# Where the first state of a chunk reads delta*x in a selective-scan kernel

## The chip, the cores and the metric

The kernel runs on one core of one Trainium2 chip. The metric is the device time of one execution in microseconds. The core has five engines that run side by side, each through its own queue in order: PE (matrix products), DVE (vector), ACT (scalar functions and copies), POOL (GpSimd, elementwise work here) and SP (which issues the DMAs). SBUF is the working memory, PSUM the small memory that PE writes to; DVE and ACT can read and write both[...].

## The reference, cut to what matters

The whole is a two-layer network on four images of 64 x 64 positions with 128 channels. The first layer begins with a selective scan over 4096 positions in four directions; the change lies there. The other parts (routing and experts, a long convolution through short transforms) run beside the scans or after them.

```python
def step(h, xs):
    ut, dt, bt, ct = xs
    dA = jnp.exp(dt[..., None] * A)
    h = dA * h + (dt * ut)[..., None] * bt[:, :, None, :]
    y = jnp.einsum('bkdn,bkn->bkd', h, ct)
    return (h, y)
```

Here `u` is x along a direction, `dt` (delta) the step size, and `h` has N = 16 states for each of 256 inner channels. The term `(dt * ut)` is delta*x: it does not depend on the state n, and each of the 16 states multiplies it by its own row of B.

## The kernel before

The sequence of an image and direction is cut into chunks of 512 positions: 4 images x 4 directions x 8 chunks are 128 chunks. A chunk lies in tiles of 128 partitions x 2 halves x 512 positions. The main loop runs over `s`, which counts (chunk, state) pairs: 128 x 16 = 2048 steps. At step `s` it emits work for several pairs at once:

- for pair s+5 the DMA of its B and C rows into `bc`, L1402, on SP;
- for pair s+3 the decay `da` = exp(delta * A), two ACT instructions, L1412;
- for pair s itself, on DVE: the product `db` = delta*x * B into PSUM, L1440, then two scans (one per half) that give `hh`, L1446. A chunk that continues a sequence starts from `hst`, the states kept from the chunk before;
- for pair s-1, on POOL: the copy of the last column to `hst`, L1455, and the product `hh` * C, L1456;
- for pair s-2, on PE: eight transposing matmuls that add up `y` in PSUM, L1482, and after the chunk's last state two ACT copies of `y`, L1352.

The step sizes of a chunk are made in pieces while the chunk before is scanned (`step_sizes`): PE L1311, ACT L1315 to L1338, POOL L1337 to L1344. They give `dl` (delta) and, as the last piece, `dx` = delta*x on POOL (L1344), in SBUF, with a single buffer. At the last state of a chunk, `into_psum` has ACT copy the next chunk's `dx` into `du` in PSUM, one copy per half (L1393). `du` has a single buffer too, so the copies can only be written when the last product of the old chunk has been read. All 16 products of a chunk read `du`:

```python
nc.scalar.copy(dus[i][:, h, :], sizes[i][1][:, h, :])                            # L1393
nc.vector.tensor_mul(db, dus[i], bcs[s][:, 0:1, :].to_broadcast([P, 2, SC]))     # L1440
```

Other work of the network is dealt out between the steps (`deal`): it is queued behind the instructions of the step at hand, a fixed share per step, and none at states 2 and 3 of a chunk. So ACT's queue holds, beside `da` and the copies, silu parts, norms and evictions of that side work. Within these limits the framework's scheduler decides the order on each engine. After the last scan comes a tail without scans: the rest of the long convolution and of the experts.

Of the kernel before, what the change touches and what calls it, by code (L numbers as in the profile page):

```python
# [17 lines left out]
P = 128  # L18
# [10 lines left out]
SC = 512  # L29
# [49 lines left out]
def kernel(  # L79
# [35 lines left out]
    nc = tc.nc  # L115
# [106 lines left out]
    def settle(leave=0):  # L222
        while len(soon) > leave:
            soon.pop(0)()
# [1030 lines left out]
    def run(pieces):  # L1255
        for _ in pieces:
            tick()
        flush()
# [3 lines left out]
    def beside(b):  # L1262

        if b == 0:
            for i in range(1, B):
                yield from before_scans(i)
            for i in range(B - 1):
                yield from gate(i)
            yield from filters()
        else:  # L1270
            yield from after_scans(b - 1)
            yield from experts_and_sums(b - 1)
            yield from to_slots(b - 1)
            if b == 1:
                yield from gate(B - 1)
            if b == B - 1:
                yield from from_slots(0)
            yield from convolve(all_groups[BESIDE * (b - 1) : BESIDE * b])

    with ExitStack() as c0:  # L1280
# [102 lines left out]
        sizes = {0: step_sizes(0, 0, 0)}  # L1383
        list(sizes[0][3])
        bcs, das, hhs, dus, hsts, ys = {}, {}, {}, {}, {}, {}
# [3 lines left out]
        def into_psum(i):  # L1389

            dus[i] = bps.tile([P, 2, SC], F32, name="du")
            for h in range(2):
                nc.scalar.copy(dus[i][:, h, :], sizes[i][1][:, h, :])  # L1393

        for s in range(-5, total + 2):
            i = max(s, 0) // N
# [22 lines left out]
            if 0 <= s < total:  # L1419
                b, k, step, _ = chunks[i]  # L1420
                n = s % N
                if n == 0:
                    if k == 0 and step == 0:
                        y_d[b] = dram.tile([K, L, DI], F32, name=f"y_d{b}")
                        if b > 0:
                            run(share["pieces"])
                            settle()
                        share = {"pieces": beside(b), "made": 0.0, "due": 0.0}
                    hsts[i] = pb.tile([P, 2, N], F32, name="hst") if step == 0 else hsts[i - 1]
                    if i == 0:  # L1430
                        into_psum(0)
                if i + 1 < len(chunks):
                    if n == 1:
                        nb_, nk, _, nci = chunks[i + 1]
                        sizes[i + 1] = step_sizes(nb_, nk, nci)
                    if n >= 1:
                        next(sizes[i + 1][3], None)
                hhs[s] = pb.tile([P, 2, SC], F32, name="hh", bufs=6)
                db = bps.tile([P, 2, SC], F32, name="db")
                nc.vector.tensor_mul(db, dus[i], bcs[s][:, 0:1, :].to_broadcast([P, 2, SC]))  # L1440
                for h in range(2):
                    init = 0.0 if step == 0 else hsts[i][:, h, n : n + 1]
                    o, d0, d1 = hhs[s][:, h, :], das[s][:, h, :], db[:, h, :]
                    if k >= 2:
                        o, d0, d1 = o[:, ::-1], d0[:, ::-1], d1[:, ::-1]
                    i_dve = nc.vector.tensor_tensor_scan(o, d0, d1, init, ALU.mult, ALU.add)  # L1446
                if n == N - 1 and i + 1 < len(chunks):
                    into_psum(i + 1)
# [14 lines left out]
            c, n = divmod(t, N)  # L1463
# [163 lines left out]
```

## Time and profile before

| what | value |
| --- | --- |
| median of 3 runs | 11200.73 us (11200.63 to 11202.45) |
| profiled execution | 11189.8 us |
| its span, first to last instruction | 11188.0 us |
| DVE busy | 8145.9 us (73% of the span) |
| POOL busy | 7262.3 us (65%) |
| PE busy | 8372.3 us (75%) |
| ACT busy | 6173.9 us (55%) |
| products L1440 | 2048, mean 1232 ns |
| scans L1446 | 3584 of mean 1266 ns and 512 of mean 1208 ns |
| copies `du` L1393 | 256, median 590 ns |
| POOL's products L1456 | 2048, mean 2359 ns |

In the profile a row of a group names line, engine, operation, output<-inputs and count, then the busy time and the mean duration of one, then how long its engine had stood idle before it and what ended most of that. The view of waits gives, for a pair of waiting and released-by instructions, the total in us, the number of times and the longest. The timeline gives start and duration in us; in brackets stands the idle time before an instruction and what ended it. Neighbouring instructions of one kind are merged.

### The profile page before, as it was taken

Reading aid. Unit: us, or ns where it says so; the run is one execution under the profiler, and the core shown is the slowest. Engines: PE = TensorE matmul, PEld = TensorE weight load, DVE = VectorE, ACT = ScalarE, POOL = GpSimd, SP = SyncE. Lnnn points to the kernel's source line nnn. Section 1 sums busy time; section 2 is a strip of 40 time slices with the busy share of each in tenths; the row PEclk is TensorE's granted clock in tenths of the full one; section 3 lists DMA queues with packets and bytes.
Section 4 is the critical chain, followed back from the end, with each engine's and each line's share of the span. In section 5 each row is a group of like instructions: output and inputs, shape, how many; then the busy total and the mean of one; then the engine's idle time right before and its main releaser. Section 6 shows DMA issues by size and latency. Waiting matters only on the chain. (4 is left out here: it accounts for less than half of the span.)

```text
span 11188.0 us, 117102 instructions
## 1 busy us (share of the span) xinstructions
PE 8372.3 (75%) x34656; PEld 4820.6 (43%) x34656; DVE 8145.9 (73%) x7046; ACT 6173.9 (55%) x12043; POOL 7262.3 (65%) x6518
## 2 busy tenths in 40 slices
PE   6677676546766777657677776576677789999999
PEld 2444443334454444444543344455344444355443
DVE  0898988887887999879878898798699933222222
ACT  4667566657566665674655566647456534124222
POOL 1878787888787878788877788778687821001001
PEclk9787777757776888778778887687788899999999
DMA  2465656657556666657565566574666664553555
GB/s 98 161 206 178 200 174 209 191 179 217 203 200 185 187 193 193 201 174 240 172 185 168 170 194 205 159 262 155 188 193 193 189 155 125 150 136 94 143 131 123
DMA packets 901458, 1980.14 MB, mean 177 GB/s; under 512 B 101563, under 2 KB 415579, under 8 KB 899291
## 3 DMA queue, kind: packets, MB, share of 16 engines
q1 hardware_dynamic: 900826, 1972.65, 58.3%
q8 instruction: 283, 4.64, 0.2%
q14 instruction: 349, 2.85, 0.1%
HBM read 1766.77 MB, written 205.52 MB: 176 GB/s over the span
## 5 line engine op out<-in xcount | busy, mean ns | idle before, releaser
L1456 POOL TENSOR_TENSOR hh<-hh,bc 128x1024 f32<-128x1024 f32 x2048 | 4829.5, 2359 | 417.4 <-DVE hh L1446 190.5
L1446 DVE TENSOR_TENSOR_SCAN hh<-da,hst,db 128x512 f32<-128x512 f32 x3584 | 4392.2, 1266 | 528.8 <-PE y L1482 146.6
L1412 ACT ACTIVATE da<-dl,aneg 128x512 f32<-128x512 f32 x4096 | 2765.3, 717 | 2006.7 <-DVE hh L1446 1922.1
L1482 PE MATMUL y<-ident,hh 128*128 128x128 f32 x16384 | 2783.7, 320 | 1092.7 <-POOL hh L1456 980.7
L1482 PEld LDWEIGHTS y<-ident,hh 128*128 128x128 f32 x16384 | 2288.6, 166 | 2452.9 <-POOL hh L1456 1290.6
L1440 DVE TENSOR_TENSOR db<-du,bc 128x1024 f32<-128x1024 f32 x2048 | 2523.2, 1232 | 733.8 <-ACT du L1393 627.3
L1142 PE MATMUL cv_ps<-slab,us 64*128 64x512 f32 x4096 | 1164.0, 674 | 528.0 <-ACT y L256 298.5
L256 ACT COPY y<-cv_ps 128x512 f32<-128x512 f32 (+1 forms) x1024 | 755.3, 742 | 687.3 <-PE cv_ps L1142 658.6
L1163 PE MATMUL zq_ps<-y,me 128*128 128x512 f32 x2048 | 1006.1, 612 | 42.5 <-ACT y L256 37.5
L1455 POOL COPY hst<-hh 128x2 f32<-128x2 f32 x1792 | 338.8, 189 | 1052.4 <-DVE hh L1446 948.1
L1163 PE MATMUL zq_ps<-y,mo 128*128 128x512 f32 x2048 | 973.1, 599 | 0.0
L254 DVE COPY y<-cv_ps 128x512 f32<-128x512 f32 x640 | 441.3, 691 | 559.5 <-PE cv_ps L1142 509.4
L1142 PEld LDWEIGHTS cv_ps<-slab,us 64*128 64x128 f32 x4096 | 398.9, 201 | 981.8 <-ACT y L256 387.2
L1179 POOL TENSOR_TENSOR zt<-zt,zt 128x512 f32<-128x512 f32 x64 | 81.2, 1269 | 1007.3 <-DVE zt L254 531.4
L1446 DVE TENSOR_TENSOR_SCAN hh<-da,db 128x512 f32<-128x512 f32 x512 | 596.9, 1208 | 64.4 <-PE y L1482 29.7
L410 PE MATMUL cv_ps<-xh,diag 128*128 128x512 f32 x1152 | 534.3, 607 | 0.9 <-ACT sg_v L352 0.8
L1163 PEld LDWEIGHTS zq_ps<-y,me 128*128 128x128 f32 x2048 | 353.4, 194 | 379.1 <-issue 266.1
L1163 PEld LDWEIGHTS zq_ps<-y,mo 128*128 128x128 f32 x2048 | 358.3, 192 | 316.2 <-issue 313.3
L1311 PE MATMUL dt_ps<-dts,dtw 8*128 8x512 f32 x512 | 352.8, 804 | 180.7 <-ACT sg_v L352 54.6
L254 DVE COPY zt<-zq_ps 128x512 f32<-128x512 f32 x39 | 26.9, 691 | 529.8 <-PE zq_ps L1163 524.2
L1337 POOL TENSOR_TENSOR ex<-ex,dx 128x1024 f32<-128x1024 f32 x128 | 302.9, 2366 | 147.1 <-ACT dx L1334 146.8
L532 PE MATMUL yk_ps<-yk,ident 128*128 128x512 f32 x512 | 278.4, 689 | 92.1 <-ACT y L256 37.6
(222 smaller groups left out, 8714.4 us busy)
## 6 DMA issues: line engine op xcount, KB each, us to landing
bc<-bc_d SPq DMA_DIRECT2D x2048, 512.0 KB
slab<-hd SPq DMA_DIRECT2D x1024, 256.0 KB
xc<-xc_d SPq DMA_DIRECT2D x128, 512.0 KB
y_d<-ys SPq DMA_DIRECT2D x128, 512.0 KB
w1t<-in_w_dram SPq DMA_DIRECT2D x128, 512.0 KB
w2t<-in_w_dram SPq DMA_DIRECT2D x256, 256.0 KB
xc_x<-xc_d SPq DMA_DIRECT2D x64, 512.0 KB
yk<-y_d SPq DMA_DIRECT2D x128, 256.0 KB
```

The lines of the kernel that those rows point to most:

```text
L254: nc.vector.tensor_copy(dst, src)
L256: nc.scalar.copy(dst, src)
L410: nc.tensor.matmul(ps, diag[:, h, t, :], xh[:, 8 * g + dy : 8 * g + dy + 8, dx : dx + W], start=(t == 0), stop=(t == 8),)
L1142: nc.tensor.matmul(pq[q].rearrange("p (r k t) -> p r k t", r=2, t=BS), us[b, G][rows, p, a if e == 0 else 1 - a, :], slab[i][rows, p, :, : ...
L1163: nc.tensor.matmul(z, (me, mo)[e][:, KQ * kq + k, :], ys[e][:, :, :, :, k, :].rearrange("p a q r t -> p (a q r) t"), start=(e == 0 and k = ...
L1311: nc.tensor.matmul(ps, dtw[:, k, h * P : (h + 1) * P], dts, start=True, stop=True)
L1412: i_act = nc.scalar.activation(das[t][:, h, :], sizes[t // N][0][:, h, :], AF.Exp, scale=aneg[:, tk, h, t % N : t % N + 1],)
L1440: nc.vector.tensor_mul(db, dus[i], bcs[s][:, 0:1, :].to_broadcast([P, 2, SC]))
L1446: i_dve = nc.vector.tensor_tensor_scan(o, d0, d1, init, ALU.mult, ALU.add)
L1455: nc.gpsimd.tensor_copy(hsts[t // N][:, :, t % N], hhs[t][:, :, last])
L1456: i_pool = nc.gpsimd.tensor_mul(hhs[t], hhs[t], bcs.pop(t)[:, 1:2, :].to_broadcast([P, 2, SC]))
L1482: i_pe = nc.tensor.matmul(ys[c][:, q, h, :], hhs[t][:, h, q * P : (q + 1) * P], ident, is_transpose=True, start=(n == 0 and k > 0 and q % ...
```

## The change

The product of a chunk's first state takes delta*x from `dx` in SBUF, where POOL made it. The products of the other 15 states read the copy `du` in PSUM as before; the copies are made as before. With the two added lines, the product stands in line 1442 and the scans in line 1448 of the kernel after.

```diff
                 hhs[s] = pb.tile([P, 2, SC], F32, name="hh", bufs=6)
                 db = bps.tile([P, 2, SC], F32, name="db")
-                nc.vector.tensor_mul(db, dus[i], bcs[s][:, 0:1, :].to_broadcast([P, 2, SC]))
+
+                src = sizes[i][1] if n == 0 else dus[i]
+                nc.vector.tensor_mul(db, src, bcs[s][:, 0:1, :].to_broadcast([P, 2, SC]))
                 for h in range(2):
```

The other lines of the loop, and the functions named above, are the same.

## The prediction

> **What bounds the kernel now.** First the busy times by stretch (span start to 297 us, six stretches of the scan stage up to 9010, then the tail; below, columns are length, then busy time and count for PE, PEld, DVE, ACT and POOL, PE clock, DMA share, GB/s). I show one quiet scan stretch, one crowded one and the tail.
>
> ```profile
> 3660.00:4680.00 1020.00, 758.27 (x3224) 430.74 (x3223) 969.66 (x795) 607.10 (x875) 827.06 (x573) 0.85 0.63 191
> 4680.00:6380.00 1700.00, 1181.54 (x5552) 756.78 (x5552) 1415.75 (x1162) 1016.57 (x2058) 1310.11 (x1205) 0.78 0.60 188
> 9010.00:11188.00 2178.00, 2111.67 (x7100) 940.25 (x7099) 541.18 (x780) 688.77 (x1625) 258.32 (x531) 0.99 0.53 133
> ```
>
> In the quiet stretch DVE works 95% of the time (969.66 of 1020), in the crowded one 83%, and no other engine reaches DVE's share in either. So the scan stage is set by DVE's line of products and scans plus what keeps DVE waiting. The tail is PE's (97% busy); it starts when the last scans are done, so time won before it shifts it whole. The chain that ended last says only this about the tail; it does not reach back into the scans.
>
> Next the view of waits, three rows of it (total us, times, longest):
>
> ```profile
> ACT da L1412 <- DVE hh L1446: 1922.1, 971, 10.3
> POOL hst L1455 <- DVE hh L1446: 948.1, 679, 17.3
> DVE db L1440 <- ACT du L1393: 627.3, 56, 286.6
> ```
>
> ACT and POOL mostly wait for DVE. DVE's own largest wait is for the copy `du`. Of its 627.3 us, 286.6 are the start of the program, before any scan; 340.7 us are 55 waits at chunk boundaries, 6.2 us each. Third, the timeline at one boundary:
>
> ```profile
> 2062.97 2.45 DVE L1446 TENSOR_TENSOR_SCAN hh<-da,hst,db 128x512 f32<-128x512 f32 x2
> ...
> 2067.37 0.60 ACT L1393 COPY du<-dx 128x512 f32<-128x512 f32 x1
> ...
> 2068.51 0.59 ACT L1393 COPY du<-dx 128x512 f32<-128x512 f32 x1
> ...
> 2069.13 1.23 DVE L1440 TENSOR_TENSOR db<-du,bc 128x1024 f32<-128x1024 f32 x1 [3.71 <-ACT du L1393]
> ...
> 2072.98 1.23 DVE L1440 TENSOR_TENSOR db<-du,bc 128x1024 f32<-128x1024 f32 x1
> ```
>
> The last scans end at 2065.42. ACT could copy from 2062.84 on (the old `du` has been read for the last time), but its queue holds side work first, so the copies come at 2067.37 and 2068.51 and DVE stands still for 3.71 us. `dx`, the source of the copies, had been finished by POOL 27.6 us before the last scans ended. From one state's product to the next is 3.85 us (2069.13 to 2072.98).
>
> [...] Today's L1440 has `du` in PSUM[...]; its durations over 2048 are 1205/1232/1233 ns (minimum, median, maximum). Two rows by shape of tiny DVE instructions whose two inputs are both in SBUF[...]:
>
> ```profile
> L626 DVE TENSOR_TENSOR left<-left,hard 128x1 f32<-128x1 f32 x4 | 5.5, 1385 | 0.0
> L629 DVE TENSOR_TENSOR wt<-wt,soft 128x4 f32<-128x4 f32 x1 | 0.1, 132 | 0.0
> ```
>
> The same kind of work costs 132 ns alone and 1385 ns when a POOL instruction is running; in the timeline each long one ends within 0.1 us of that POOL instruction's end, although POOL's next already stands in its queue. [...] No run here shows the new form at this size.
>
> **The change, part by part.** The counts and the operations stay. Only the first product of each of 128 chunks is touched.
>
> *1. The first product's wait goes.* I read, off DVE's and ACT's timelines, when the second `du` copy ended after the last scan at each of 127 boundaries:
>
> - 70 on time: nothing to win.
> - 20 late by up to 3.85 us, together 46.4 us: all of it can be won.
> - 37 late by more, together 355.6 us: here the second product, which still reads `du`, becomes the one that waits. At most one state, 3.85 us, is won: 37 x 3.85 = 142.5.
>
> Sum: 46.4 + 142.5 = 188.9 us of 402. (402 exceeds 340.7 because at five boundaries small routing instructions lie on DVE inside the wait.) What is late next: `dx` itself and `da`. `dx` ends 9 to 47 us before the last scan everywhere but at boundaries 81 to 88, where POOL ends it 1.0 to 7.0 us after; with that and the `da` of the first state counted, some 187 remain.
>
> *2. The port.* At each boundary I took the POOL instruction running when the last scan ends (or `dx` is ready) and let the product wait for its end, as the tiny instructions do. On-time boundaries: 15 of 70 hit, 10.7 us together, longest 1.9. Late ones: 29 us, most of it hidden since the second product waits for `du` anyway. The gain falls from about 187 to **165 us**. Where POOL starts the little `hst` copy (0.19 us) in the same instant, as it does 0.02 to 0.03 us after the product at on-time boundaries, I assume DVE first; bound 0 to 70 x 0.25 = 17 us, or a whole product (2.36) more if POOL slips it in between, which is the rival below.
>
> *3. POOL waits behind the product.* Up to 1.23 us per boundary. Queued behind it are `hst` and the output product L1456, for which PE's transposes wait. POOL needs 0.19 + 2.35 = 2.54 of a state's 3.85 us, so it makes this good in one state. Cost 0, covered by POOL's 948.1 us of waiting for DVE; bound 128 x 1.23 = 157 us if that cover were gone.
>
> *4. The product's own time.* [...] I take 0.
>
> *5. Buffers and queues.* `dx` has one buffer; its next writer is ACT L1334 of the next chunk, now also behind the first product. In the boundary at 2003.85 that writer came at 2021.57, 17.7 us later: cost 0. The 256 copies of 0.59 us stay on ACT, and `du`'s last reader is still state 15. No DMA is added, and none of SP's work is passed by the edit. In the built order the scheduler places about a quarter of the chunks' step-size work (L1311 to L1344) one or two states later (chunk 32: five), still at least five states ahead of its boundary except where it was late already, and ten of the 256 copies half a state to a state away, mostly earlier. I cost this at 0, bound 20 us either way.
>
> *6. What is kept.* A gain stays only if the late copy follows DVE. I walked back from each late copy through what released it. At 47 of 61 boundaries with over 0.3 us of waiting the walk ends at a scan of the chunk just before (states 1 to 14), that is, at work which moves earlier with DVE. The rest end at a DMA, at older work, or can't be followed, and at the five with routing instructions the product stays behind these in DVE's order. I keep three quarters: 0.75 x 165 = 124 us.
>
> **Sum.** The profiled execution took 11189.8 us (span 11188.0, 1.8 around it), 11 us below the median 11200.7. Its span should fall to about 11064; from the median, 11200.7 - 124 = about **11076 us**, 1.1% faster.
>
> **Rivals.**
>
> *The port decides (slower).* [...] Before the port, 0.75 x 187 = 140 us would be won; over 127 boundaries it is gone when a boundary costs 1.1 us more. If POOL's `hst` and L1456 pass first at every on-time boundary, 70 x 2.6 = 182 us are lost, and with 124 won elsewhere the time is about 11259. Against it: waiting instructions got in after one POOL instruction in the trace, and POOL waits for the same scan end as DVE. For it: POOL is 83% busy in the first scan stretch. Chance 0.10.
>
> *The wait only moves.* If the side work's own chain (PE, POOL, DMA) sets when the copy comes, the next boundary is later by what was won. The walk speaks against it, the 14 that do not end at a near scan for it. With under a tenth of 188.9 kept: 11180 to 11201. Chance 0.08. A scheduler that undid the edit would give 11201 too, but the built order has 128 first products that read `dx`, so I give that no chance of its own.
>
> **How the numbers follow.** Main case 0.82. Low end: all 187 kept, without port losses: about 11010. High end: 0.1 x 188.9 kept: about 11180, which takes in half of the case where the wait moves. A measurement of this kernel can tell 0.2%, 22 us, from no change. Faster 0.82, same 0.08, slower 0.10.
>
> **What would show it.** Right: the wait for `du` falls from 340.7 (without the start) to some 215 us and stands before a state's second product; first products sit 0.1 us behind the last scan; their durations reach from 1.2 to about 3.6 us, with some 50 us in all over 1232 ns; a new small wait for `dx` at boundaries 81 to 88. Wrong: first products mostly over 2.4 us, POOL's L1456 lengthened at the boundaries with DVE waiting for `hh` buffers after it, or boundaries late by as much as before.

## The result and the profile after

| | median | range |
| --- | --- | --- |
| before, 4 runs | 11200.68 us | 11198.13 to 11202.45 |
| after, 4 runs | 11129.69 us | 11127.63 to 11149.03 |

The ratio is 0.9941 with an interval of [0.9929, 0.9954]. The change wins 71 us; 124 were forecast. Measured a second time, the same kernel gave 0.9945 [0.9933, 0.9958].

The two profiled executions understate this: that of after took 11149.0 us and is the slowest of its four, while that of before is 11 us below its median. So I also use the profile of the second measurement (below "the repeat", 11130.9 us).

First the same three stretches as before, in the profile after: length, busy time and count of PE, PEld, DVE, ACT and POOL, then PE clock, DMA share and GB/s.

```profile
3660.00:4680.00 1020.00, 773.51 (x3192) 433.40 (x3191) 963.56 (x786) 604.44 (x874) 832.29 (x568) 0.83 0.64 189
4680.00:6380.00 1700.00, 1194.63 (x5627) 757.24 (x5626) 1455.72 (x1179) 1028.97 (x2072) 1345.03 (x1214) 0.78 0.61 190
9010.00:11147.00 2137.00, 2081.81 (x7028) 928.10 (x7026) 535.07 (x771) 679.47 (x1603) 257.20 (x525) 0.99 0.53 132
```

In the crowded stretch DVE's share rises from 83% to 86% (1455.72 of 1700), in the quiet one it is as it was. From the end of the last scan to the end of the program are 2178.7 us, against 2180.8 before: the tail was moved whole.

Next the view of waits of after: total us, times, longest.

```profile
DVE db L1442 <- POOL dx L1344: 313.9, 9, 282.7
DVE hh L1448 <- PE y L1484: 210.5, 62, 20.7
DVE db L1442 <- ACT du L1393: 143.3, 33, 13.2
DVE hh L1448 <- ACT da L1412: 85.0, 38, 7.4
```

The wait for `du` fell from 340.7 (without the start) to 143.3 us, and each of its 31 waits of over 0.2 us stands before the second product of a chunk. The 282.7 us of the `dx` row are the start of the program; the other 31.2 are eight waits, at boundaries 81 to 88 exactly. But DVE's scans wait longer than before for PE (210.5; 176.3 before) and for `da` (85.0; 79.5).

The two rows of the products, on the page of after:

```profile
L1442 DVE TENSOR_TENSOR db<-du,bc 128x1024 f32<-128x1024 f32 x1920 | 2365.8, 1232 | 247.2 <-ACT du L1393 143.3
L1442 DVE TENSOR_TENSOR db<-dx,bc 128x1024 f32<-128x1024 f32 x128 | 222.4, 1738 | 322.6 <-POOL dx L1344 313.9
```

A product that reads `dx` takes 1738 ns in the mean, and so 128 x 0.506 = 64.7 us more than the same products with `du`. In the scan stage, from the first product to the end of the last scan, DVE's idle time falls by 98.4 us (1110.0 to 1011.6) and its busy time rises by 64.0 (7600.2 to 7664.2): the stage is 34.4 us shorter in this profile. In the repeat it is 49.6 us shorter.

The timeline of DVE in after, at the boundary that was shown of before:

```profile
2043.22 2.45 DVE L1448 TENSOR_TENSOR_SCAN hh<-da,hst,db 128x512 f32<-128x512 f32 x2
2045.71 2.06 DVE L1442 TENSOR_TENSOR db<-dx,bc 128x1024 f32<-128x1024 f32 x1
2047.91 2.45 DVE L1448 TENSOR_TENSOR_SCAN hh<-da,hst,db 128x512 f32<-128x512 f32 x2
2051.26 1.23 DVE L1442 TENSOR_TENSOR db<-du,bc 128x1024 f32<-128x1024 f32 x1 [0.90 <-ACT du L1393]
```

And POOL's:

```profile
2044.33 2.36 POOL L1458 TENSOR_TENSOR hh<-hh,bc 128x1024 f32<-128x1024 f32 x1
2046.64 2.26 POOL L499 TENSOR_TENSOR sg_v<-sg_v,sg_e 128x512 f32<-128x512 f32 x1
```

The first product now follows the scans at once. It is recorded as 2.06 us: POOL's `hh` product runs until 2046.69, and the product ends 1.1 us after that. POOL's next instruction in turn, of a kind that takes 1.28 us in the median of this stretch, is drawn out to 2.26 us and ends 1.1 us after the product, as it would if it waits for the product. What is left of the wait for `du` is 0.90 us where it was 3.71.

### The profile page after: what moved, and what is told of

The parts are those of the page before. It is cut to its first block, busy times and chain, and to the rows that moved or that the text cites. A ratio compares the mean times of both kernels' runs of the same rounds, so it can differ in the third digit from the quotient of the medians.

```text
span 11147.2 us, 117203 instructions
## 1 busy us (share of the span) xinstructions
PE 8390.8 (75%) x34656; PEld 4830.0 (43%) x34656; DVE 8210.0 (74%) x7046; ACT 6171.3 (55%) x12043; POOL 7377.5 (66%) x6518
## 5 line engine op out<-in xcount | busy, mean ns | idle before, releaser
L1442 DVE TENSOR_TENSOR db<-du,bc 128x1024 f32<-128x1024 f32 x1920 | 2365.8, 1232 | 247.2 <-ACT du L1393 143.3
L1457 POOL COPY hst<-hh 128x2 f32<-128x2 f32 x1792 | 410.9, 229 | 890.7 <-DVE hh L1448 787.2
L1448 DVE TENSOR_TENSOR_SCAN hh<-da,db 128x512 f32<-128x512 f32 x512 | 597.1, 1208 | 58.7 <-PE y L1484 22.0
L1442 DVE TENSOR_TENSOR db<-dx,bc 128x1024 f32<-128x1024 f32 x128 | 222.4, 1738 | 322.6 <-POOL dx L1344 313.9
```

What stands on the lines that cost most here:

```text
L1442: nc.vector.tensor_mul(db, src, bcs[s][:, 0:1, :].to_broadcast([P, 2, SC]))
L1457: nc.gpsimd.tensor_copy(hsts[t // N][:, :, t % N], hhs[t][:, :, last])
```

## The experiments

In the diffs "-" is the kernel after, unless said otherwise. Each result stands against the kernel before, measured beside it (medians 11194.7 to 11196.6 us). "Boundary" below is the time from the end of a chunk's last scan to the start of the next chunk's second product, and "inside" is the rest of the chunk; the gain of each is its time in before less its time in the experiment, all from the timelines. A chunk's first product (state 0) is the one that the change touches. "The port" is a name, as in the prediction, for the delay that the timelines of after show at the boundary above: where a product with both inputs in SBUF meets a POOL instruction, one of the two, mostly the later, takes longer (2.06 us in place of 1.23 for the product, 2.26 in place of 1.28 for POOL's). What in the hardware makes this delay was not shown. "Without the port" is a product with one input in PSUM: the 1920 that read `du` in after take 1208 to 1233 ns.

### The same cover without the port

```diff
-                db = bps.tile([P, 2, SC], F32, name="db")
-                src = sizes[i][1] if n == 0 else dus[i]
+                if n == 0 and i > 0:
+                    db = dbs
+                else:
+                    db = dbs = bps.tile([P, 2, SC], F32, name="db")
+                src = db if n == 0 and i > 0 else dus[i]
```

> The product of a chunk's first state (but the first chunk's) reads, in place of delta*x, the old contents of its own output tile in PSUM: it is as free to start as in the change, but has one SBUF input only. The first state's B*delta*x term is left wrong. Theory A[...]: faster than the change by a good part of the 65 us by which its 128 first products lasted over 1232 ns (222.4 us against 157.7), so 11065 to 11100 us; first products all at 1.2 us. Theory B (the port is hidden, side work takes the gain back): 11120 to 11135 us, the same as the change.

Measured: 11093.05 us, 0.9908 [0.9894, 0.9921], 103 us won, as the first theory expected. These first products are not lengthened by POOL, as their row by shape in this kernel's profile shows:

```profile
L1444 DVE TENSOR_TENSOR db<-db,bc 128x1024 f32<-128x1024 f32 x127 | 156.5, 1232 | 6.6 <-DMA bc<-bc_d 2.3
```

So of the 187 us that the prediction allowed before the port, 103 are kept even where there is no port: 0.55 of them. The change itself is slower by another 37 to 41 us (0.9908 against 0.9941 and 0.9945, of 11197 us). Most of that is the port, but not all: at boundaries 81 to 88 the change's first product waits for `dx`, which the product in place does not, and 5 to 6 us of the difference arise at these eight (29.3 us won there in place, 23.4 and 24.0 by the change and its repeat).

### The port without the cover

```diff
-                src = sizes[i][1] if n == 0 else dus[i]
+                src = sizes[i][1] if n == 1 else dus[i]
```

> The second state's product reads dx in SBUF, the first state's reads du as before: the port's price without any earlier start, result unchanged. Theory A: the extra time at on-time boundaries of the change, 29 us over 70, is 0.4 us each; at 128 products that is about 53 us, so 11240 to 11260 us. Theory B (a delayed product is made good elsewhere): 11195 to 11210 us.

Measured: 11227.82 us, 1.0028 [1.0018, 1.0039], 31 us slower than before, between the two expectations. The row of the products that read `dx`:

```profile
L1442 DVE TENSOR_TENSOR db<-dx,bc 128x1024 f32<-128x1024 f32 x128 | 184.2, 1439 | 7.3 <-DMA bc<-bc_d 2.1
```

They take 26.5 us over 1232 ns together; the longest lasts 9.3 us. The boundary waits are nearly as in before (347.6 us for `du`, without the start; 340.7 there), so most of the 31 us is what the read from SBUF costs on DVE, and little of POOL's own delay came back to it.

### Reading `dx` only where the copy had been late

```diff
-                src = sizes[i][1] if n == 0 else dus[i]
+                src = sizes[i][1] if n == 0 and i in LATE else dus[i]
```

`LATE` is a written list of 55 chunks whose copy was late in the profile of before.

> Only 55 chunks, those whose copy was over 1 us late (two between 0.4 and 1 us are left out) in the profile of before, read dx for their first product; the other 73 read du throughout. Theory A: the 28 us that the change lost at the 70 on-time boundaries come back: about 11100 us. Theory B: nothing comes back, 11125 to 11135 us. Below 11090 or above 11140 speaks against both.

Measured: 11121.75 us, 0.9932 [0.9918, 0.9945], between the two expectations and near the second. It is the fastest of the kernels here that leave the computation whole, but its interval overlaps that of the change: the two can't be told apart. The profile does show the on-time boundaries relieved. They lose 9.7 us in all where the change loses 27.9, and the products that read `dx` take 31.9 us too much in place of 64.7.

### No boundary waits for a copy at all

"-" is the kernel before.

```diff
-            dus[i] = bps.tile([P, 2, SC], F32, name="du")
+            if i == 0:
+                dus[i] = bps.tile([P, 2, SC], F32, name="du")
+            else:
+                dus[i] = dus[0]
+                away = pb.tile([P, SC], F32, name="du2", bufs=1)
...
-                nc.scalar.copy(dus[i][:, h, :], sizes[i][1][:, h, :])
+                nc.scalar.copy(dus[i][:, h, :] if i == 0 else away, sizes[i][1][:, h, :])
```

> All products read one du in PSUM that was copied for the first chunk; the later chunks' 254 copies are still made by ACT, but into an SBUF tile that nobody reads. The values of delta*x are left wrong for all but the first chunk. No product waits for a copy[...]. In the profile of before the copies were late by 402 us in all. Theory A (three quarters of a removed wait are kept): 10890 to 10910 us. Theory B (side work takes back more than half): 11000 to 11060 us, with longer waits of the scans for da, for PE's transposes and for bc.

Measured: 11046.39 us, 0.9865 [0.9851, 0.9878], 150 us won, as the second theory expected. All 402 us of lateness are out of DVE's way, and 150 us are won. The waits of this kernel:

```profile
DVE db L1444 <- ACT du L1397: 289.3, 1, 289.3
DVE hh L1450 <- PE y L1486: 289.3, 77, 22.9
DVE hh L1450 <- ACT da L1416: 156.8, 68, 10.9
ACT du L1397 <- POOL dx L1344: 411.9, 80, 9.3
```

The wait for `du` is the start of the program and nothing else. In its place the scans wait 113 us longer for PE (176.3 before) and 77 us longer for `da` (79.5 before). The edit changes ACT too: the copies need not wait for the old chunk's last product any more and start a median 13.6 us before its end, where ACT then waits 411.9 us for `dx`; in before it waits at no copy for `dx`. How much of the wait for `da` comes from that was not separated, so the 150 us need the next experiment beside them, which leaves the copies where they are.

### Two states covered without the port, and the change again

The edit is that of the first experiment with `n < 2` in place of `n == 0`.

> The first two states' products read the old contents of their output tile in PSUM (but in the first chunk); their delta*x term is left wrong. No port, and up to two states of a late copy are covered: of 402 us at most 46 + 37 x 3.85 + 118 = 307 us, against 189 with one state (11093 us, 103 us won) and 402 with no wait at all (11046 us, 150 us won). Theory A (a fixed share of what is uncovered is kept, 0.55): 0.55 x 307 = 169 us won, about 11030 us. Theory B (the lateness of ACT and PE itself is the limit, what is uncovered beyond a first part only moves into the waits for da and for PE): 115 to 140 us won, 11055 to 11085 us.

> The changed kernel once more, on the chip of the next three, so that they can be held against it. Both theories: 0.994 of before, about 11130 us. A second profile shows whether the product of 14.3 us at chunk 112 is a single event: if it comes from the built order of POOL's queue it comes again, if it is chance of the moment it does not.

Measured: two states covered give 11040.89 us, 0.9862 [0.9847, 0.9877], 154 us won, between the two expectations (169, and 115 to 140); the change again 11135.01 us, as expected. The second covered state adds 51 us to the first one's 103, and the kernel in which no product waits for a copy (the experiment before this one) wins no more. The waits with two states covered:

```profile
DVE hh L1450 <- PE y L1486: 266.3, 69, 22.2
DVE hh L1450 <- ACT da L1412: 105.7, 48, 10.9
```

At the boundaries 384 us are won in this kernel, and 236 of them are lost again inside the chunks. Of the 236 us, 90 are longer waits of the scans for PE, 62 are the wait for `du`, which now stands before the third product, and 39 are DVE's small routing instructions and the waits for them, which had lain in the boundaries before; the wait for `da` is only 7 us longer there (and 19 at the boundaries).

### Side work kept off the last states of a chunk

`BUSY` lists the states at which no side work is dealt out. One kernel is before, the other the change, each with this edit:

```diff
-BUSY = (2, 3)
+BUSY = (13, 14)
```

> The kernel before, with the two states to which no side work is dealt moved from states 2 and 3 to states 13 and 14 of each chunk. Theory A (the copy is late because of side work dealt just ahead of it in ACT's queue): the lateness falls to well under half of 402 us, the wait for du below 170 us, and the time to 11050 to 11130 us. Theory B (the lateness comes from chains several states long, whatever lies just ahead): du waits about as before, and the time is within 40 us of 11197, either way, as the step sizes made in states 2 and 3 now meet side work.

> The changed kernel with the same two states moved. Theory A: the two edits win from the same lateness, so it is no more than 15 us faster than the moved states alone (or slower, by the port). Theory B: the change wins about what it wins on its own, 60 to 75 us, against the kernel with the moved states alone.

Measured: before with the edit 11205.62 us, 1.0009 [1.0003, 1.0016]; the change with it 11139.16 us, 0.9947 [0.9935, 0.996]. Both times are those of the second theory, though the wait for `du` falls further than it had it. Before's copies come less late (274 us in place of 402), yet the time is no shorter. The waits of before with the edit:

```profile
DVE db L1440 <- ACT du L1393: 547.0, 61, 287.7
DVE hh L1446 <- PE y L1482: 251.4, 65, 23.2
DVE hh L1446 <- ACT da L1412: 125.1, 50, 8.4
```

The wait for `du` is 81 us shorter (259.3 without the start); those for PE and `da` are 75 and 46 us longer. Here the shorter wait at the boundary was worth nothing. The edit also puts side work on states 2 and 3, so it does not show by itself that the wait can't be removed with profit. The change still wins 66 us on top of this edit, as much as without it.

### Two states from `dx`

The first kernel has `n < 2` in place of `n == 0`; the second picks the chunks:

```diff
-                src = sizes[i][1] if n == 0 else dus[i]
+                early = n == 0 and i in LATE or n == 1 and i in VERY
+                src = sizes[i][1] if early else dus[i]
```

`VERY` are the 37 chunks that were late by more than one state.

> The first two states of every chunk read dx in SBUF. Without the port, covering two states won 154 us against 103 for one; the port took some 35 us from the change and 31 us from the kernel where only state 1 used it. Theory A (the port's price adds up state by state): 154 - 35 - 31 = 88 us won, about 11107 us. Theory B (with more cover the port's waits hide behind what is late anyway): 110 to 150 us won, 11045 to 11085 us.

> The first state reads dx in the 55 late chunks, the second state too in the 37 of them whose copy was over 3.85 us late in the profile of before; all others read du. Result unchanged. Theory A (the port is paid only where it buys something): most of the 154 us, less some 20 us of port: 11055 to 11075 us, faster than the change and than two states everywhere. Theory B (selection buys nothing, as the late chunks hold the port's price too): within 10 us of two states everywhere.

Measured: 11152.99 us (0.9959 [0.9945, 0.9973]) and 11123.75 us (0.9934 [0.9922, 0.9947]). Neither came where it was expected: the first wins 44 us, less than the change, and the second no more than reading `dx` once per late chunk. Their rows of products from `dx`, the first kernel's and then the second's:

```profile
L1442 DVE TENSOR_TENSOR db<-dx,bc 128x1024 f32<-128x1024 f32 x256 | 415.7, 1624 | 327.8 <-POOL dx L1344 317.0
```

```profile
L1447 DVE TENSOR_TENSOR db<-dx,bc 128x1024 f32<-128x1024 f32 x92 | 159.0, 1728 | 36.5 <-POOL dx L1348 32.1 <-DMA bc<-bc_d 0.8
```

Over 1232 ns these are 100.3 and 45.7 us. The kernel to hold them against is the one that covers two states without the port: they are 109 and 81 us slower than it (0.9959 and 0.9934 against 0.9862). The longer products are the larger part of that. A second part arises at boundaries 81 to 88, where `dx` itself is late: the products in place do not wait for it and win 53.7 us there, the two kernels here 25.7 and 25.2. Without what the long products there account for (10.7 us in each), this is 17 and 18 us. Together the two parts cover the first kernel's loss (117 us against 109) and most of the second's (64 against 81). The waits for PE (233.8 and 257.0 us) are not longer than in the kernel without the port (266.3), so they do not explain it. A cover that reads `dx` can't start before `dx` is made, and both expectations had left that out.

## Why the prediction was right, and what was mis-sized

The direction, the place and the mechanism were right: a wait before the first product became a shorter wait before the second, and the tail moved with the scans. The size was 71 us of 124. The balance of the scan stage, in us (waits without the program's start; "in place" and "no copy awaited" are the kernels of the experiments):

| | before | after | repeat | in place, one state | in place, two | no copy awaited |
| --- | --- | --- | --- | --- | --- | --- |
| length | 8710.2 | 8675.8 | 8660.6 | 8605.9 | 8562.0 | 8568.9 |
| DVE busy | 7600.2 | 7664.2 | 7664.2 | 7596.7 | 7597.9 | 7598.7 |
| DVE idle | 1110.0 | 1011.6 | 996.4 | 1009.2 | 964.2 | 970.2 |
| product for `du` | 341 | 143 | 138 | 164 | 62 | 0 |
| product for `dx` | 0 | 31 | 32 | 0 | 0 | 0 |
| scan for PE's `y` | 176 | 211 | 223 | 217 | 266 | 289 |
| scan for `da` | 80 | 85 | 86 | 83 | 106 | 157 |

**Step 1, the wait that goes.** 188.9 us were counted at the boundaries. Without the port 154 came (119 of 142.5 at the 37 late by more than a state, 34 of 46.4 at the 20 late by less). At the 37, the first state's scans, which had waited for neither, now waited 19.8 us for `da` and 12.3 for PE. That `dx` would be late at boundaries 81 to 88 only was right. The wait for `du` was to fall to some 215 us and fell further, to 143, while the time fell by less than forecast: the total of a wait is not time won.

**Step 2, the port.** Too low. The price was put at 22 us of the gain before step 6; it is some 31 to 36 us of the time (the 37 to 41 less what arises at boundaries 81 to 88). The on-time boundaries lose 27.9 us (30.5 in the repeat) and not 10.7. All but one of the delayed products wait for the end of one POOL instruction, as assumed: 50 of 128 take over 1.35 us, and 49 of these at most 3.38, a POOL product of 2.36 and a part of their own. Each ends 1.09 or 1.10 us after the end of a POOL instruction. (The tiny instruction of 132 ns that the prediction calls alone was not: it started 0.03 us before the end of a POOL instruction. One that had none beside it, at 2312.48 in the trace of before, took 0.13 us too, so the reading stands.) The step's bound for the `hst` copy was not needed either. The timeline of DVE at an on-time boundary of after, then POOL's:

```profile
1001.88 1.25 DVE L1442 TENSOR_TENSOR db<-dx,bc 128x1024 f32<-128x1024 f32 x1
```

```profile
1001.97 1.20 POOL L1457 COPY hst<-hh 128x2 f32<-128x2 f32 x1
```

DVE goes first and the small copy lasts 1.20 us in place of 0.19. About 13 of the 27.9 us are one product that broke the step's rule, at chunk 112 in the timeline of after, all engines:

```profile
7952.37 2.78 POOL L1245 TENSOR_TENSOR xr<-xr,iv 64x256 f32<-64x256 f32 x4
...
7954.27 14.34 DVE L1442 TENSOR_TENSOR db<-dx,bc 128x1024 f32<-128x1024 f32 x1
...
7955.10 4.67 POOL L1458 TENSOR_TENSOR hh<-hh,bc 128x1024 f32<-128x1024 f32 x2
...
7959.73 2.77 POOL L1245 TENSOR_TENSOR xr<-xr,iv 64x256 f32<-64x256 f32 x4
7962.45 2.35 POOL L1458 TENSOR_TENSOR hh<-hh,bc 128x1024 f32<-128x1024 f32 x1
...
7964.74 2.77 POOL L1245 TENSOR_TENSOR xr<-xr,iv 64x256 f32<-64x256 f32 x4
```

The product ends at 7968.61, 1.1 us after POOL's row of instructions has ended at 7967.5. It started while the third of POOL's first four was running, and twelve that began after it went past it (the fourth of these and the eleven in the rows below): 13 us are lost in one place. The repeat has it too, at the same chunk:

```profile
7936.92 14.31 DVE L1442 TENSOR_TENSOR db<-dx,bc 128x1024 f32<-128x1024 f32 x1
```

**Step 3, POOL behind the product.** POOL's `hst` row carries the waiting, on the page of after:

```profile
L1457 POOL COPY hst<-hh 128x2 f32<-128x2 f32 x1792 | 410.9, 229 | 890.7 <-DVE hh L1448 787.2
```

The mean rises from 189 to 229 ns, 72 us in all, and POOL's wait for DVE falls from 948.1 to 787.2: the cover that the step named was used. Without the port, in place, that wait is 858.7, so about half of the fall belongs to the port. With the port alone 31 us were lost and 26.5 were DVE's own, so at most some 5 us of POOL's delay reached DVE there.

**Step 4, the product's own time.** Right at zero: in the list of the line's durations the median is 1234 ns with both inputs in SBUF and 1232 with one in PSUM.

```profile
L1442 DVE TENSOR_TENSOR db<-du,bc x1920: 1208/1232/1233, 297.0 to 8964.7; 128x1024 f32<-128x1024 f32 x192
L1442 DVE TENSOR_TENSOR db<-dx,bc x128: 1216/1234/14343, 292.7 to 8906.9; 128x1024 f32<-128x1024 f32 x128
```

**Step 5, buffers and queues.** No cost was seen, and none could be separated: the built order also differs a little between all these kernels.

**Step 6, what is kept.** This is the term that was mis-sized most: 0.75 was assumed, and 0.55 was measured without the port. Three quarters were kept because the walk back from late copies ended, at 47 of 61, at a scan of the chunk before. That showed what a late copy had last waited for, not that the other engines keep up with a faster DVE. Against the last scan the copies came later than before: they are 464 us late in after (461 in the repeat) where they were 402. And of the 154 us won at the boundaries without the port, 50 were lost inside the chunks; with the port it is 99 won and 49 lost in the repeat. In the profile without the port the scans wait 31 us longer for PE inside the chunks and 18 us longer for POOL's norm steps; for `da` they wait 18 us less there, after 22 us more at the boundaries, which the 154 has in it already. Some 9 us are routing instructions and their waits, which had lain at the boundaries.

Uncovering more gives less and less: 187 us of cover gave 103, two states without the port gave 154, the whole 402 gave 150. So past some 150 us something else than the copies sets the time. The waits that grow most are those for PE's `y`, behind the six `hh` buffers. That PE, or POOL whose products PE waits for, is the limit fits the waits but was not tested: neither more `hh` buffers nor an earlier `da` was tried.

**The rivals.** "The port decides" named a real cost and gave it too much weight: POOL does not win at every on-time boundary; mostly DVE does (of all 128 first products, 78 take at most 1.35 us). "The wait only moves" is in part what happened: not all of the gain went, but nearly half of it even without the port, and in good part to waits for PE.

## What to carry to other kernels

A stall that is taken off the busiest engine need not be won in full: before the gain is counted, look for the next waits of that engine and let an experiment take the stall away entirely, which here gave 150 us of 402, and see in its trace what else the edit moved. A product like this one, an elementwise instruction on DVE whose inputs both lie in SBUF, has to be priced with what POOL runs beside it, mean and longest (in after 1738 ns and 14.34 us, against 1232 ns with one input in PSUM), and so belongs at those steps where the wait that it removes is longer. (The kernel that reads `dx` only in late chunks does so; it could not be told apart from the change.)

## What was unexpected in the hardware

In after all but one of the delayed products wait for one POOL instruction: 49 of the 50 last at most 3.38 us and end 1.09 or 1.10 us after the end of a POOL instruction. An `hst` copy behind a product lasts up to 1.245 us. But at chunk 112 a waiting product was passed by twelve POOL instructions in a row (14.34 and 14.31 us in two profiles of the same kernel). Chunk 112 stands out in every kernel in which one of its products reads `dx`: 9.3 us with the port alone, 14.1 with two states from `dx`, 11.5 in the change with the side work moved. So it is not chance of the moment. One other product was passed by more than a small copy, 6.5 us at chunk 48 with two states from `dx`. What sets these apart from the boundaries where POOL also ran on without a gap stays open.
